# Three small clears behind each indirect transfer of a sparse MoE kernel

## The chip, the cores and the metric

The kernel runs on one core of a Trainium2 chip. The metric is the device time of one execution in microseconds (us). Where several runs are given, their median counts.

## What is computed

The input x has 2048 tokens of 256 numbers in float32. Two layers follow each other, and each has a feed-forward part before and after its middle part, added with half weight:

- Layer 0: a mixture of experts (8 experts with 176 hidden units, the best 2 for each token, and a shared expert), then a time mix and a channel mix, then the mixture again.
- Layer 1: a mixture of experts (32 experts with 96 hidden units, the best 6, and a shared expert), then attention with rotary angles over two sequences of 1024 tokens, then the mixture again.

One mixture, cut down from the reference:

```
scores = softmax(x @ gate_w);  topk_w, topk_idx = top_k(scores, K)
g = silu(x @ w_gate[e]) * (x @ w_up[e])            # for each expert e of a token
routed = sum over e of comb[t, e] * (g @ w_down[e])
shared = silu(x @ sw_gate) * (x @ sw_up) @ sw_down
out = routed + shared
```

In layer 1 the scores are sigmoids, and the K weights are scaled to a sum of one.

## The kernel before

The tokens lie in 16 tiles x0 to x15 of 128 rows, which stay in SBUF from start to end. The work is a sequence of mixtures with other parts between them. The two mixtures of layer 0, named L0_0 and L0_1, take all 16 tiles. Those of layer 1 are cut into halves A (tiles 0 to 7) and B (tiles 8 to 15): L1_0A, L1_0B, L1_1A, L1_1B. The profile shortens these names, to L, L_0A and so on.

A mixture computes only the chosen pairs of token and expert. Its steps, all functions inside `sparse_moe`:

1. `ready(g)`, for each of two groups of tiles: `prep` normalizes the tiles, transposes them, and picks experts; `plan` counts and gives every pair a slot (`idx`), so that slots of one expert lie together in blocks of 128; `scatter` writes each token's row to its slots in a DRAM tensor `xs`, with one indirect transfer of 128 rows (128 KB) for every tile and every k, issued by GpSimd (POOL).
2. `owners` and `weights` find which expert owns each block, and the weight of each pair.
3. `shared` computes the shared expert for a range of tiles.
4. `blocks` runs over the blocks (39 in layer 0, 79 in each half of layer 1). `fetch` loads a block of `xs` through SP's queue, and waits for all writes of step 1; `features` transposes it, `inner` and `outward` are the expert's matmuls (lines 600 and 617), and SP stores the result to a DRAM tensor `ys` (line 626).
5. `combine` reads the results back: `gather` issues, for each tile and k, one indirect transfer of 128 rows from `ys` into a tile `yk` (8 buffers) on POOL (line 636), and `add_back` adds it to x on DVE (line 647), four transfers later. A read for a tile of the first group needs the first 23 (layer 0) or 55 (layer 1) blocks to be stored, one for the second group needs all.

The parts overlap: the blocks of one half run while the other half's tokens are read back, attended and written. At the end nothing is left beside the reads of L1_1B but the last blocks.

There are 512 indirect transfers: 256 that write slots (32 + 32 + 4 x 48) and 256 that read (the same numbers). POOL does little else: constants and three zero tiles at line 282, and 32 additions to x in layer 0 (lines 829 and 851). An indirect transfer waits on POOL for its indices or for the blocks' stores; POOL takes its instructions in the order in which they stand in its queue.

The order of instructions on each engine is made by a scheduler, which simulates the program with costs of its own (`tc.block(schedule_with_timeline_sim=True)`), so a change can move instructions of other engines too. `tc.issue_after(x)` is a hint to it: what is issued inside stands behind x. It adds no wait on the chip.

Of the kernel before, what the change touches and what calls it, by code (L numbers as in the profile page):

```python
# [8 lines left out]
F32 = mybir.dt.float32  # L9
# [5 lines left out]
P = 128  # L15
# [24 lines left out]
def moe_blocks(m, tiles=NT):  # L40
    return (tiles * P * m["K"] + m["E"] * (P - 1)) // P
# [3 lines left out]
def macaron_kernel(ctx: ExitStack, tc: tile.TileContext, a: dict, out: bass.AP):  # L45
    nc = tc.nc
    ctx.enter_context(tc.block(schedule_with_timeline_sim=True))

    const = ctx.enter_context(tc.tile_pool(name="const", bufs=1))
# [220 lines left out]
    def load_down(w, layer, lo, n):  # L270
# [5 lines left out]
            ),  # L276
        )

    def fill_slots(xs, n, behind=None):

        zero = const.tile([P, D], F32, tag="zero", name=f"zero_{n}")
        nc.gpsimd.memset(zero, 0.0)
        d = nc.sync.dma_start(
            out=xs.rearrange("(n p) d -> p n d", p=P),
            in_=zero.unsqueeze(1).to_broadcast([P, n, D]),
        )
        if behind is not None:
            tc.add_manual_dep(d.ins, behind.name, SYNC, reason="not beside the blocks' loads")
# [6 lines left out]
    def sparse_moe(layer, w, name, first_tile, tiles, xs, ys, moe, last=False):  # L295
# [14 lines left out]
        idx = back.tile([P, tiles, K], I32, tag="idx", name=f"idx_{name}", bufs=2)  # L310
# [5 lines left out]
        def places(t):  # L316

            h, i = divmod(t, HT)
            if h not in xn:
                xn[h] = moe.tile([P, HT, D], F32, tag="xn", name=f"xn_{name}_{h}", bufs=2)  # L320
                xT[h] = moe.tile([P, DC, SEQ], F32, tag="xT", name=f"xTs_{name}_{h}", bufs=2)
            return xn[h], xT[h], i
# [109 lines left out]
        def scatter(g):  # L432

            for t in range(GT * g, GT * g + GT):
                xb, _, i = places(t)
                for k in range(K):
                    d = nc.gpsimd.indirect_dma_start(  # L437
                        out=xs,
                        out_offset=bass.IndirectOffsetOnAxis(ap=idx[:, t, k : k + 1], axis=0),
                        in_=xb[:, i, :],  # L440
                        in_offset=None,
                    )
                    tc.declare_no_dep(
                        d.ins, group=f"slots_{name}", reason="a slot is one pair's"
                    )
                    tc.add_to_no_dep_group(f"slots_{name}", d.ins)
                    scattered.append(d.ins)
# [183 lines left out]
        def gather(t, k):  # L631

            yk = back.tile([P, D], F32, tag="yk", name=f"yk_{name}_{t}_{k}", bufs=8)

            n = first if t < GT else NBLK
            d = nc.gpsimd.indirect_dma_start(  # L636
                out=yk,
                out_offset=None,
                in_=ys[0 : n * P, :],
                in_offset=bass.IndirectOffsetOnAxis(ap=idx[:, t, k : k + 1], axis=0),  # L640
            )
            for s in stored[0:n]:
                tc.add_manual_dep(d.ins, s.name, SYNC, reason="the blocks are done")
            gathered[t, k] = yk
# [10 lines left out]
        def combine(t0, t1, lag=4):  # L655

            pairs = [(t, k) for t in range(t0, t1) for k in range(K)]
            for n in range(len(pairs) + lag):
                if n < len(pairs):
                    gather(*pairs[n])  # L660
                if n >= lag:
                    add_back(*pairs[n - lag])
                yield
# [16 lines left out]
        def ready(g):  # L680

            for b in range(GT // BT * g, GT // BT * (g + 1)):
                prep(b)
            plan(g)
            scatter(g)
# [329 lines left out]
    xs, ys = {}, {}  # L1015
    for k, layer, tiles in (("L0", "L0", NT), ("A", "L1", HT), ("B", "L1", HT)):
        n = moe_blocks(MOE[layer], tiles)
# [8 lines left out]
    def rest_of_x():  # L1026
        for b in range(1, NB):
            load_x(b)
        fill_slots(xs["L0"], moe_blocks(MOE["L0"]))
# [8 lines left out]
    with tc.tile_pool(name="rwkvw", bufs=1) as weights:  # L1038
        with tc.tile_pool(name="moe_L0_0", bufs=1) as pool:
            m = sparse_moe("L0", w0, "L0_0", 0, NT, xs["L0"], ys["L0"], pool)  # L1040
            m["ready"](0)
            m["ready"](1)
            m["owners"]()
            load_rwkv(weights)
            m["weights"](0)
            m["weights"](1)
            m["shared"](0, HT)
            m["shared"](HT, NT)
            blocks = m["blocks"]()
            for n, _ in enumerate(blocks):  # L1050
                if n == m["first"] + 4:
                    break
            all_of(m["combine"](0, HT), blocks)
        all_of(m["combine"](HT, NT))
        for k in ("A", "B"):
            fill_slots(xs[k], moe_blocks(MOE["L1"], HT), behind=m["latest"]["add"])
        with tc.tile_pool(name="rwkv", bufs=1) as pool:
            rw["pool"] = pool
            run(rwkv)
# [121 lines left out]
```

## Time and profile before

| what | value |
|---|---|
| three runs | 1573.4, 1567.35 and 1575.41 us |
| median | 1573.4 us |
| profiled execution, own time | 1867.49 us |
| its span | 1865.7 us |
| granted clock of TensorE, mean | 0.814 |
| indirect transfer on POOL | 0.95 to 0.97 us, and 0.30 us until the next |
| POOL busy | 521.9 us (28%), 560 instructions |

The profiled execution is 294 us longer than the median of the timed runs. The profile names the engines PE (TensorE), PEld (its weight loads), DVE (VectorE), ACT (ScalarE), POOL (GpSimd) and SP. A row of a timeline has start and length in us, engine, line, operation, written and read tiles and shapes, and in brackets the idle time before it and what ended it. "remote", and "another core or an unknown queue" in the chain of waits, mean that the profile found nobody who ended the wait. The profile gives one execution, and the ends of matmuls in it are modelled.

### The profile page before, as it was taken

Reading aid. Unit: us, or ns where it says so; the run is one execution under the profiler, and the core shown is the slowest. Engines: PE = TensorE matmul, PEld = TensorE weight load, DVE = VectorE, ACT = ScalarE, POOL = GpSimd, SP = SyncE. Lnnn points to the kernel's source line nnn. Section 1 sums busy time; section 2 is a strip of 40 time slices with the busy share of each in tenths; the row PEclk is TensorE's granted clock in tenths of the full one; section 3 lists DMA queues with packets and bytes.
Section 4 is the critical chain, followed back from the end, with each engine's and each line's share of the span. In section 5 each row is a group of like instructions: output and inputs, shape, how many; then the busy total and the mean of one; then the engine's idle time right before and its main releaser. Section 6 shows DMA issues by size and latency. Waiting matters only on the chain.

```text
span 1865.7 us, 23891 instructions
## 1 busy us (share of the span) xinstructions
PE 1392.4 (75%) x6460; PEld 1080.6 (58%) x6460; DVE 763.6 (41%) x2586; ACT 660.8 (35%) x1796; POOL 521.9 (28%) x560
## 2 busy tenths in 40 slices
PE   6799767999879964634499758559778549788971
PEld 5577534566667743424398636449645439667960
DVE  5223368453322342233244554424446324344443
ACT  4133357775313330210154313126323216434520
POOL 1500331011060037236302340630540440342054
PEclk8699878999769975765699877679888559898985
DMA  9403339000720332172166420246631135555653
GB/s 280 162 27 107 105 124 371 18 1 0 155 85 29 105 93 101 68 200 79 62 187 184 135 60 23 96 137 187 172 96 31 65 107 179 175 158 165 186 173 102
DMA packets 204987, 223.54 MB, mean 120 GB/s; under 512 B 42268, under 2 KB 187836, under 8 KB 204860
## 3 DMA queue, kind: packets, MB, share of 16 engines
q1 hardware_dynamic: 180284, 154.87, 27.3%
q0 software_dynamic: 24576, 67.14, 11.5%
q8 instruction: 59, 0.97, 0.2%
q14 instruction: 68, 0.56, 0.1%
HBM read 108.81 MB, written 113.12 MB: 119 GB/s over the span
## 4 chain that ended last, share of the span: by engine, by line
PE 59%; another core or an unknown queue 13%; DVE 10%; issue 8%; ACT 5%; DMA 3%; POOL 1%; SPq 0%; POOLq 0%; DVEq 0%; ACTq 0%
PE pg_L_b L600 5%; PE pg_L L513 4%; PE py_L_b L617 3%; PE pkv_cm L761 3%; PE pg_L_1A_b L600 3%; PE pg_L_1B_b L600 3%; PE pg_L_0B_b L600 3%; PE pg_L_0A_b L600 3%; PE py_L L554 2%; PE pkk_cm L749 2%; PE py_L_1A_b L617 2%; PE py_L_1B_b L617 2%; PE py_L_0B_b L617 2%; PE py_L_0A_b L617 2%
## 5 line engine op out<-in xcount | busy, mean ns | idle before, releaser
L636 POOL DMA_INDIRECT yk_L<-ys_L,idx_L x64 | 62.2, 972 | 316.7 <-DMA ys_L<-yb_L 263.2
L600 PE MATMUL pg_L_b<-L0gu,xbT_L 128*128 x312 | 111.2, 481 | 0.0
L513 PE MATMUL pg_L<-L0sgu,xTs_L 128*128 128x352 f32 x256 | 99.1, 523 | 2.5 <-DVE h_L L504 2.5
L617 PE MATMUL py_L_b<-L0down,hT_L_b 88*128 x312 | 86.7, 403 | 10.6 <-ACT hT_L_b L536 6.2
L636 POOL DMA_INDIRECT yk_L_0A<-ys_A,idx_L_0A x48 | 46.1, 961 | 147.3 <-DMA ys_A<-yb_L_0A 103.2
L437 POOL DMA_INDIRECT xs_L<-xn_L,idx_L x64 | 61.7, 964 | 80.8 <-DVE wk_L L498 34.8
L617 PEld LDWEIGHTS py_L_b<-L0down,hT_L_b 88*128 88x128 f32 x312 | 62.2, 202 | 33.8 <-ACT hT_L_b L536 7.6
L636 POOL DMA_INDIRECT yk_L_1A<-ys_A,idx_L_1A x48 | 45.8, 954 | 124.4 <-DMA ys_A<-yb_L_1A 78.2
L636 POOL DMA_INDIRECT yk_L_0B<-ys_B,idx_L_0B x48 | 46.6, 970 | 121.0 <-DMA ys_B<-yb_L_0B 79.3
L504 DVE TENSOR_TENSOR h_L_b<-g_L_b,pg_L_b 128x176 f32<-128x176 f32 x78 | 26.2, 336 | 130.7 <-ACT g_L_b L503 104.9
L636 POOL DMA_INDIRECT yk_L_1B<-ys_B,idx_L_1B x48 | 46.0, 959 | 111.3 <-DMA ys_B<-yb_L_1B 89.4
L600 PE MATMUL pg_L_1A_b<-L1gu,xbT_L_1A 128*128 x316 | 69.9, 347 | 4.3 <-issue 3.9
L600 PE MATMUL pg_L_0B_b<-L1gu,xbT_L_0B 128*128 x316 | 70.5, 349 | 3.5 <-issue 3.1
L437 POOL DMA_INDIRECT xs_A<-xn_L_1A,idx_L_1A x48 | 46.7, 973 | 83.8 <-DVE same_L_1A L491 69.8
L437 POOL DMA_INDIRECT xs_B<-xn_L_1B,idx_L_1B x48 | 46.4, 967 | 81.9 <-DVE same_L_1B L491 67.8
L600 PE MATMUL pg_L_1B_b<-L1gu,xbT_L_1B 128*128 x316 | 68.8, 343 | 0.1
L600 PE MATMUL pg_L_0A_b<-L1gu,xbT_L_0A 128*128 x316 | 67.9, 339 | 0.2 <-PE ph_L_0A_b L529 0.2
L513 PEld LDWEIGHTS pg_L<-L0sgu,xTs_L 128*128 128x128 f32 x256 | 52.3, 219 | 26.1 <-issue 9.6
L600 PEld LDWEIGHTS pg_L_b<-L0gu,xbT_L 128*128 128x128 f32 x312 | 56.2, 199 | 18.4 <-issue 2.5
L536 ACT COPY hT_L_b<-ph_L_b 88x256 f32<-88x256 f32 x78 | 28.6, 369 | 103.7 <-PE ph_L_b L529 50.1
L617 PE MATMUL py_L_0B_b<-L1down,hT_L_0B_b 96*128 x158 | 51.5, 409 | 17.6 <-issue 11.9
L749 PE MATMUL pkk_cm<-mk_cm,w_WkeyT 128*128 128x512 f32 x128 | 60.8, 606 | 3.1 <-ACT sk_cm L841 3.1
(593 smaller groups left out, 3583.4 us busy)
## 6 DMA issues: line engine op xcount, KB each, us to landing
xs_A<-zero SPq DMA_DIRECT2D x1, 10112.0 KB
xs_B<-zero SPq DMA_DIRECT2D x1, 10112.0 KB
xb_L_0A<-xs_A SPq DMA_DIRECT2D x79, 128.0 KB
ys_A<-yb_L_0A SPq DMA_DIRECT2D x79, 128.0 KB
xb_L_0B<-xs_B SPq DMA_DIRECT2D x79, 128.0 KB
ys_B<-yb_L_0B SPq DMA_DIRECT2D x79, 128.0 KB
xb_L_1A<-xs_A SPq DMA_DIRECT2D x79, 128.0 KB
ys_A<-yb_L_1A SPq DMA_DIRECT2D x79, 128.0 KB
```

Source lines behind the costliest of these rows:

```text
L437: d = nc.gpsimd.indirect_dma_start(out=xs, out_offset=bass.IndirectOffsetOnAxis(ap=idx[:, t, k : k + 1], axis=0), in_=xb[:, i, :], in_offs ...
L504: nc.vector.tensor_tensor(dst, g, pg[:, width : 2 * width], ALU.mult)
L513: nc.tensor.matmul(pg, xbT[:, c, i * P : (i + 1) * P], w["sgu"][:, c, u, :, :].rearrange("p z w -> p (z w)"), start=(c == 0), stop=(c == D ...
L536: nc.scalar.copy(hT[0:m, lo:hi, :].rearrange("p k t -> p (k t)"), pt[0:m, lo * P : hi * P])
L554: nc.tensor.matmul(py, hT[0:m, k, :], w["sdown"][0:m, k, :], start=(k == 0), stop=(k == len(rows) - 1),)
L600: nc.tensor.matmul(pg, xbT[:, c, :], w["gu"][:, c, bass.ds(e, 1), :, :].rearrange("p e z h -> p (e z h)"), start=(c == 0), stop=(c == DC - 1),
L617: nc.tensor.matmul(py, hT[0:HP, k, :], w["down"][:, bass.ds(e, 1), k, :].rearrange("p e d -> p (e d)"), start=(k == 0), stop=(k == C - 1),)
L636: d = nc.gpsimd.indirect_dma_start(out=yk, out_offset=None, in_=ys[0 : n * P, :], in_offset=bass.IndirectOffsetOnAxis(ap=idx[:, t, k : k + ...
L749: nc.tensor.matmul(ps, w[:, c, oc * P : (oc + 1) * P], src[:, c, :], start=(c == 0), stop=(c == DC - 1),)
L761: nc.tensor.matmul(ps, src[:, c, i * P : (i + 1) * P], w[:, c, :], start=(c == 0), stop=(c == n - 1),)
```

## The change

A tile `pause` of 128 x 128 float32 is added. A helper `spaced` puts three clears of it on POOL behind each indirect transfer, and asks the scheduler to put the next transfer of the same kind (same mixture, and for writes the same group) behind the third. The writes of all mixtures go through it, and the reads of all but L1_1B.

```diff
+    pause = const.tile([P, P], F32, tag="pause", name="pause")
+
+    pauses = {}
+
+    def spaced(of, d):
+
+        if of in pauses:
+            with tc.issue_after(pauses[of]):
+                d = d()
+        else:
+            d = d()
+        with tc.issue_after(d.ins):
+            for _ in range(3):
+                pauses[of] = nc.gpsimd.memset(pause, 0.0).ins
+        return d
...
-                    d = nc.gpsimd.indirect_dma_start(
+                    d = spaced(("xs", name, g), lambda: nc.gpsimd.indirect_dma_start(
                         out=xs,
                         out_offset=bass.IndirectOffsetOnAxis(ap=idx[:, t, k : k + 1], axis=0),
                         in_=xb[:, i, :],
                         in_offset=None,
-                    )
+                    ))
...
-            d = nc.gpsimd.indirect_dma_start(
-                out=yk,
-                out_offset=None,
-                in_=ys[0 : n * P, :],
-                in_offset=bass.IndirectOffsetOnAxis(ap=idx[:, t, k : k + 1], axis=0),
-            )
+
+            def row():
+                return nc.gpsimd.indirect_dma_start(
+                    out=yk,
+                    out_offset=None,
+                    in_=ys[0 : n * P, :],
+                    in_offset=bass.IndirectOffsetOnAxis(ap=idx[:, t, k : k + 1], axis=0),
+                )
+
+            d = row() if name == "L1_1B" else spaced(("yk", name), row)
```

## The prediction

> **What bounds the kernel now.** I read the busy times and the chain of waits on the page first, then the stages by windows, then the timeline of one stage with many indirect transfers. In the page, PE carries the chain, and a line of the chain has no owner:
>
> ```profile
> span 1865.7 us, 23891 instructions
> PE 1392.4 (75%) x6460; PEld 1080.6 (58%) x6460; DVE 763.6 (41%) x2586; ACT 660.8 (35%) x1796; POOL 521.9 (28%) x560
> PE 59%; another core or an unknown queue 13%; DVE 10%; issue 8%; ACT 5%; DMA 3%; POOL 1%; SPq 0%; POOLq 0%; DVEq 0%; ACTq 0%
> ```
>
> There is one core, so 13% of 1865.7, 243 us, are waits that the profile cannot explain. The windows show where they lie (columns: PE, PEld, DVE, ACT, POOL busy, clock, DMA share, GB/s):
>
> ```profile
> 685.00:765.00 80.00, 33.19 (x130) 25.80 (x128) 22.90 (x120) 10.06 (x15) 48.46 (x51) 0.52 0.25 87
> 950.00:1000.00 50.00, 50.00 (x321) 46.40 (x320) 21.39 (x72) 27.36 (x107) 0.00 (x0) 1.00 0.62 190
> 1250.00:1300.00 50.00, 50.00 (x320) 45.19 (x319) 23.84 (x71) 31.33 (x107) 0.00 (x0) 1.00 0.61 186
> ```
>
> Where POOL issues nothing, PE is busy all of the time at full clock. Where POOL issues indirect transfers back to back, PE does 33 us of work in 80. The timeline of such a burst:
>
> ```profile
> 745.65 2.07 PE L617 MATMUL py_L_b<-L0down,hT_L_b 88*128 x4 [3.93 <-issue]
> ...
> 747.94 2.55 PE L600 MATMUL pg_L_b<-L0gu,xbT_L 128*128 x4
> ...
> 755.48 0.96 POOL L437 DMA_INDIRECT xs_A<-xn_L_0A,idx_L_0A  x1 [0.30 <-issue]
> 756.46 0.42 DVE L625 COPY yb_L<-py_L_b 128x256 f32<-128x256 f32 x1 [9.70 <-remote]
> 756.75 0.96 POOL L437 DMA_INDIRECT xs_A<-xn_L_0A,idx_L_0A  x1 [0.31 <-issue]
> ...
> 766.26 0.32 ACT L503 ACTIVATE g_L_b<-pg_L_b 128x176 f32<-128x176 f32 x1 [19.36 <-remote]
> ```
>
> DVE may copy py_L_b when its matmuls end at 747.7 and starts at 756.5; ACT may read pg_L_b at 750.5 and starts at 766.3. Counted over the timeline, a DVE or ACT instruction that needs a matmul's result starts more than 1 us late 63 times of 280 inside bursts and 5 times of 1317 outside; the late stretches together cover 284 us. Now the timed runs: the profiled execution took 1867.5 us, the median is 1573.4, 294 less. PE idles 1865.7 - 1392.4 = 473 us in the profile; a run of 1573 has room for 181 us of idling, and 473 - 284 is 189. I read this so: **the late starts belong to the profiled execution and are nearly all absent when the kernel is timed.** The trace's own records say the same: inside bursts it holds 429 semaphore events for 774 DVE instructions, outside 1530 for 1485. [...] So the sum below is made on the profile with the late starts taken out.
>
> [...] the row of 740.29 ends at 741.25, its semaphore rises at 742.52. [...]
>
> **The change part by part.** It adds 3 memsets behind 464 of the 512 indirect transfers: 256 writes to xs_* and 208 reads of ys_*; the 48 reads of sequence 1B stay. That is 1392 memsets. POOL's rows for the same shape:
>
> ```profile
> 1.39 0.20 POOL masks.py:65 MEMSET before<- 128x128 f32 x1
> 1.53 0.19 POOL L80 MEMSET every<- 128x128 f32 x1
> ```
>
> They start 0.14 us apart and take 0.20 each. In the program as built each memset also waits for the semaphore of the one before it. Three cost at least 3 x 0.14 = 0.42 us; at most 3 x (0.20 + 0.10) = 0.90 with a tenth for each wait. I take 0.14 + 2 x 0.20 = 0.54, about 0.55, since the first can start in the 0.30 us that POOL leaves idle behind each transfer. The interval of a burst is 0.96 + 0.30 = 1.27 us and becomes **1.82 us** (1.69 to 2.17). POOL gains 1392 x 0.2 = 278 us of work beside 522: it is never full over the span, so only ends of bursts count. Stage by stage:
>
> - First writes of L0_0 (32, from 40 us) end at 40 + 32 x 1.82 = 98 instead of 89.5. Shared-expert matmuls cover them to about 131 in the profile, 113 without 18 us of late starts: 0. L0_1 (32, from 513): 571 instead of 560.5; cover to 598 - 25 = 573, and data need 2 us to land: +0 (+11 at 2.17). In both, the built order puts the first write of group 1 ahead of the last four of group 0, so POOL waits there for group 1's indices; they are ready by then.
> - Reads of L0 before the time mix: the 16 late ones end 9 us later, at 277; POOL's first add behind them ran at 292. +2 for DVE's queue.
> - **From L0 to L1.** 16 reads from 667.6 end at 697 instead of 687.5; then 48 writes to xs_A, of which the built order puts 13 behind a read that needs the last L0 block. PE's blocks end at 800, of which 41 us are late starts between 685 and 765, so near 763. SP then loads L1down and attention weights for 23 us before the first xb_L_0A, so PE resumes at about 787. (In the built order SP's first nine loads of xb_L_0A move behind all eight turn tables, some 5 us, which the wait for the reads hides.) After: idx at 704, 35 writes to 768, one read, 13 writes to 793, then 15 reads to 821. Preparing half B needs 8 reads (808, against 790) and then all 16 (824, against 820 from its own pace): +18 and +4. **+22** (15 to 47).
> - Reads of 0A and 0B: 24 for group 0, then 24 for group 1, which attention's second half needs. For 0A, without late starts: group 0 from 1013.5 to 1057; group 1 may start at 1058 and ends at 1102 instead of 1088; with landing, adding and normalizing, 1108 against 1096, when PE is done with the first half. **+12 to 13 each, 26 together** (16 to 56).
> - Nothing for the writes of 0B, 1A and 1B and the reads of 1A: 112 us of block matmuls (79 x 1.42) stand between them and their use. If that cover went, each would cost 48 x 0.55 = 26 us.
>
> The sum is 0 + 2 + 22 + 26 = 50 us, 33 at the low price, about 119 at the high one. On the median: 1573.4 + 50 = **1623.4 us**.
>
> **Rivals.** *Faster, by fewer late starts.* If the timed run holds some of them, which needs PE's half-clock stretches to be faster there, the 189 us of other idling could shrink and leave up to 100 us of late starts. A first late start comes some 14 us into a burst (212 in the one from 197.6, 1028 in the one from 1013.5), as if something filled up; 0.55/1.82 = 30% fewer transfers per time could empty it. Then perhaps 60 of 100 us come back, and late starts being cover, only 30 of the 50 are paid: 1543 us. It decides once more than 50 us come back. For it: the burst is the only thing all late starts share. Against: the arithmetic of 294 and 284 us.
> *No change.* The scheduler sees the memsets and orders around them (PE has some 300 lines of difference in 5430 instructions), and the two exposed places shrink to a few us: 1578 us. Against: POOL's order of transfers is nearly the same, and PE's order at the two places too.
> *High price.* If each memset pays its semaphore in full, 2.17 us: 1692 us.
> *Not done as said.* The scheduler could have collected the memsets elsewhere; the built order has three between nearly all pairs, so this is left out. Less strain on the shared DMA engines brings nothing: PE is full at a DMA share of 0.62.
>
> **How the numbers follow.** Slower by the sum, 0.60; high price, 0.10; no change, 0.07; faster, 0.23. The likeliest's own range is 1600 to 1660. The range of 1540 to 1680 leaves out the best of the faster cases and the worst of the slow ones, about 2 in 10. 0.5% is 8 us, about what the three runs spread (8.06), and all that a measurement here can tell.
>
> **What would show it.** In the profile after, intervals in bursts of 1.8 us with three memset rows; xs_A's writes broken by a read and ending 30 us later against the gathers before; PE waiting for pt_L_0B and for the second pt_at group. The profiled execution itself may well get shorter[...], while the timed run gets longer. If the timed run gets shorter, the late starts were real, and the reading of 294 us is wrong; if nothing moves, the covers are longer than I put them.

## The result, and the profile after

| runs | before, median us | after, median us | ratio of after to before (95%) |
|---|---|---|---|
| the pair that gives the result (4 runs each) | 1571.81 | 1674.03 | 1.0654 [1.0622, 1.0686] |

On chips like the one that ran this pair, the change makes the kernel 102 us slower: the predicted direction, and a loss twice the forecast of 50 us. Its profiled execution took 1673.05 us, as much as its timed runs; that of the kernel before had taken 1867.49 against a median of 1573.4.

The head of the page after, its chain by engine, and the row of the clears (busy us, mean ns | idle before):

```profile
span 1671.3 us, 25279 instructions
...
PE 1336.4 (80%) x6460; PEld 1045.6 (63%) x6460; DVE 767.9 (46%) x2586; ACT 665.4 (40%) x1796; POOL 818.9 (49%) x1952
...
PE 54%; DMA 15%; DVE 10%; POOL 9%; issue 6%; ACT 4%; SPq 2%; POOLq 0%; DVEq 0%; ACTq 0%
...
L292 POOL MEMSET pause<- 128x128 f32 x1392 | 292.7, 210 | 54.0
```

"Another core or an unknown queue" has gone from the chain; DMA and POOL have taken 12 and 8 points more. Not all of this is the change: the experiments show that the two profiles are of chips of different kinds. The windows of two bursts of 48 writes (columns as before), xs_A of L1_0A and xs_B of L1_1B:

```profile
669.00:764.00 95.00, 50.05 (x222) 38.24 (x222) 29.86 (x123) 17.03 (x44) 78.15 (x193) 0.70 0.49 148
1334.00:1424.00 90.00, 83.22 (x499) 74.48 (x498) 48.84 (x183) 46.63 (x151) 75.58 (x189) 0.90 0.63 200
```

In the second, PE works through the burst (83 of 90 us busy). In the first it still has a hole (50 of 95), and the waits say why (us in total, times, longest):

```profile
PE pt_at L148 <- DVE axl_at L139: 51.3, 2, 26.3
PE px_L_0A L594 <- DMA xb_L_0A<-xs_A: 43.4, 2, 42.7
PE pt_L_0A L148 <- DVE xn_L_0A L139: 19.8, 2, 16.2
PE pt_L_0B L148 <- DVE xn_L_0B L139: 15.7, 2, 12.7
```

These are not late starts but waits for the end of a burst: the first block of L1_0A for the last write to xs_A, and the second half of attention, twice, for the reads of 0A and of 0B. Counted as in the prediction, a start over 1 us late comes 2 times in 903 inside bursts, where it was 63 in 280; here too the chips differ. The price of three clears, in POOL's timeline: a burst of writes, then one of reads:

```profile
699.21 0.97 POOL L453 DMA_INDIRECT xs_A<-xn_L_0A,idx_L_0A  x1 [0.16 <-issue]
700.18 0.74 POOL L292 MEMSET pause<- 128x128 f32 x3
701.09 0.97 POOL L453 DMA_INDIRECT xs_A<-xn_L_0A,idx_L_0A  x1 [0.16 <-issue]
...
940.88 0.95 POOL L654 DMA_INDIRECT yk_L_0A<-ys_A,idx_L_0A  x1 [0.50 <-issue]
941.83 0.74 POOL L292 MEMSET pause<- 128x128 f32 x3
943.07 0.95 POOL L654 DMA_INDIRECT yk_L_0A<-ys_A,idx_L_0A  x1 [0.50 <-DVE h_L_0A_b L520]
```

A write now starts 1.88 us after the one ahead, a read 2.19; the prediction took 1.82 for both. In place of 0.30 us of idling stand 0.74 + 0.16 = 0.90 behind a write and 0.74 + 0.50 = 1.24 behind a read, so three clears cost 0.60 and 0.94 us.

### The profile page after: what moved, and what is told of

It reads as the page before. It is cut to its first block, busy times and chain, and to the rows that moved or that the text cites. A ratio compares the mean times of both kernels' runs of the same rounds, so it can differ in the third digit from the quotient of the medians.

```text
span 1671.3 us, 25279 instructions
## 1 busy us (share of the span) xinstructions
PE 1336.4 (80%) x6460; PEld 1045.6 (63%) x6460; DVE 767.9 (46%) x2586; ACT 665.4 (40%) x1796; POOL 818.9 (49%) x1952
## 4 chain that ended last, share of the span: by engine, by line
PE 54%; DMA 15%; DVE 10%; POOL 9%; issue 6%; ACT 4%; SPq 2%; POOLq 0%; DVEq 0%; ACTq 0%
PE pg_L_b L616 5%; PE pg_L L529 4%; POOL pause L292 4%; PE py_L_b L633 4%; PE pkv_cm L781 3%; DMA yk_L<-ys_L,idx_L 3%; PE py_L L570 3%; PE pg_L_1A_b L616 3%; DMA yk_L_1A<-ys_A,idx_L_1A 2%; PE pg_L_0B_b L616 2%; DMA yk_L_0B<-ys_B,idx_L_0B 2%; PE pkk_cm L769 2%; PE pg_L_0A_b L616 2%; DMA yk_L_0A<-ys_A,idx_L_0A 2%; PE pg_L_1B_b L616 2%
## 5 line engine op out<-in xcount | busy, mean ns | idle before, releaser
L292 POOL MEMSET pause<- 128x128 f32 x1392 | 292.7, 210 | 54.0
L529 PE MATMUL pg_L<-L0sgu,xTs_L 128*128 128x352 f32 x256 | 92.9, 499 | 3.8 <-DVE h_L L520 3.8
L633 PE MATMUL py_L_b<-L0down,hT_L_b 88*128 x312 | 81.8, 385 | 0.0
L520 DVE TENSOR_TENSOR h_L_b<-g_L_b,pg_L_b 128x176 f32<-128x176 f32 x78 | 26.2, 336 | 95.4 <-ACT g_L_b L519 95.1
L616 PE MATMUL pg_L_0B_b<-L1gu,xbT_L_0B 128*128 x316 | 66.3, 333 | 0.5 <-issue 0.2
L616 PE MATMUL pg_L_1A_b<-L1gu,xbT_L_1A 128*128 x316 | 65.6, 331 | 0.8 <-PE ph_L_1A_b L545 0.7
L594 PE MATMUL px_L_0A<-ident,xb_L_0A 128*128 128x128 f32 x158 | 30.9, 280 | 43.4 <-DMA xb_L_0A<-xs_A 43.4
L654 POOL DMA_INDIRECT yk_L_1A<-ys_A,idx_L_1A x48 | 46.7, 973 | 36.6 <-DMA xb_L_1A<-xs_A 12.4
L667 DVE SCALAR_TENSOR_TENSOR x<-yk_L,wk_L,x 128x256 f32<-128x256 f32 x64 | 30.8, 481 | 70.6 <-DMA yk_L<-ys_L,idx_L 70.2
```

The costliest lines, as they stand in the source:

```text
L292: pauses[of] = nc.gpsimd.memset(pause, 0.0).ins
L520: nc.vector.tensor_tensor(dst, g, pg[:, width : 2 * width], ALU.mult)
L529: nc.tensor.matmul(pg, xbT[:, c, i * P : (i + 1) * P], w["sgu"][:, c, u, :, :].rearrange("p z w -> p (z w)"), start=(c == 0), stop=(c == D ...
L594: nc.tensor.transpose(px[:, c * P : (c + 1) * P], xb[:, c * P : (c + 1) * P], ident)
L616: nc.tensor.matmul(pg, xbT[:, c, :], w["gu"][:, c, bass.ds(e, 1), :, :].rearrange("p e z h -> p (e z h)"), start=(c == 0), stop=(c == DC - 1),
L633: nc.tensor.matmul(py, hT[0:HP, k, :], w["down"][:, bass.ds(e, 1), k, :].rearrange("p e d -> p (e d)"), start=(k == 0), stop=(k == C - 1),)
```

## The experiments

All variants edit the helper `spaced`; most leave some transfers without clears:

```diff
     def spaced(of, d):
 
+        if not (<the transfers that keep their clears>):
+            return d()
         if of in pauses:
```

In these runs the kernel before turned out to have two times, by the chip that ran it, and the ratio always compares runs of one chip:

| set, chip | kernel | before us | this us | ratio (95%) |
|---|---|---|---|---|
| 1, chip 12 | e1_covered: writes 0B, 1A, 1B, reads 1A | 1855.98 | 1724.17 | 0.9272 [0.9246, 0.9298] |
| 1, chip 12 | e2_turn: reads L0_1, writes L1_0A | 1855.98 | 1836.33 | 0.9901 [0.9867, 0.9936] |
| 1, chip 12 | e3_attend: reads L1_0A, L1_0B | 1855.98 | 1868.96 | 1.0065 [1.0041, 1.0088] |
| 1, chip 12 | e4_layer0: writes and reads L0_0, writes L0_1 | 1855.98 | 1823.80 | 0.9829 [0.9805, 0.9853] |
| 2, chip 13 | e5_after: the whole change | 1572.35 | 1674.69 | 1.0661 [1.0595, 1.0726] |
| 2, chip 13 | e6_one: one clear, not three | 1572.35 | 1566.64 | 0.9970 [0.9951, 0.9989] |
| 2, chip 13 | e8_before: the kernel before, profiled | 1572.35 | 1568.43 | one run |
| 3, chip 9 | e9_spared: all but those of e2 and e3 | 1574.11 | 1590.20 | 1.0098 [1.0059, 1.0136] |
| 3, chip 9 | e10_one: one clear | 1574.11 | 1567.33 | 0.9949 [0.9930, 0.9967] |
| 3, chip 9 | e11_attend: as e3 | 1574.11 | 1625.34 | 1.0301 [1.0248, 1.0355] |
| 3, chip 9 | e12_after: the whole change | 1574.11 | 1675.88 | 1.0635 [1.0593, 1.0677] |
| 4, chip 2 | e13_turn: as e2 | 1867.96 | 1850.28 | 0.9914 [0.9885, 0.9943] |

### The change cut into four places

```diff
# e1_covered
+        if not (of[:2] in (("xs", "L1_0B"), ("xs", "L1_1A"), ("xs", "L1_1B"), ("yk", "L1_1A"))):
# e2_turn
+        if not (of[:2] in (("yk", "L0_1"), ("xs", "L1_0A"))):
# e3_attend
+        if not (of[:2] in (("yk", "L1_0A"), ("yk", "L1_0B"))):
# e4_layer0
+        if not (of[:2] in (("xs", "L0_0"), ("yk", "L0_0"), ("xs", "L0_1"))):
```

> Clears only behind the 192 transfers that I held to be covered by block matmuls: the writes of L1_0B, L1_1A, L1_1B and the reads of L1_1A. Place theory (a longer burst is paid only where something waits for its end): 0 to +8 us against the kernel before. Rival, price per transfer wherever it lies [...]: 102 us x 192/464 = +42. In the profile, late starts vanish from these four bursts and stay in the others, so the profiled execution should come out roughly midway between 1867 and 1673 us while the timed runs stay near 1572.

> Clears only behind the 80 transfers of the passage from layer 0 to layer 1: the reads of L0_1 and the writes of L1_0A. Place theory with the waits of the profile after (PE stands 16, 5, 43, 13 and 5 us there, part of which the kernel before has too): +35 to +50 us; the prediction's own term was +22. Rival, price per transfer: 102 x 80/464 = +18.

> Clears only behind the 96 reads of L1_0A and L1_0B, ahead of attention. Place theory with the two waits for pt_at of 25 and 26 us in the profile after: +35 to +52 us; the prediction's own term was +26. Rival, price per transfer: 102 x 96/464 = +21.

> Clears only behind the 96 transfers of L0_0 (writes and reads) and the writes of L0_1. Place theory: +2 by the prediction, up to +20 by the four waits of PE of 25 us in all around the time mix in the profile after. Rival, price per transfer: 102 x 96/464 = +21. If places add up without touching each other, the four kernels of this set sum to the +102 us of the whole change.

All four expectations fell, and with them a premise of mine. The 13 runs of the kernel before took 1851 to 1865 us here: what I had thought a property of one profiled execution is the usual time here. There the clears behind the covered bursts gained 132 us, those of the turn 20 and of layer 0 32, and only attention's reads lost 13. Here is the profile of e1_covered, head and chain, and the windows of three bursts of 48 writes, of which the first (to xs_A of L1_0A) has no clears and the others (xs_B of L1_1B and of L1_0B) have them:

```profile
span 1730.1 us, 24471 instructions
...
PE 60%; DVE 9%; issue 8%; DMA 8%; another core or an unknown queue 6%; ACT 5%; POOL 2%; SPq 2%; DVEq 0%; POOLq 0%; ACTq 0%
```

```profile
704.00:766.00 62.00, 23.96 (x85) 17.50 (x85) 15.35 (x82) 3.09 (x5) 46.57 (x48) 0.53 0.29 104
1378.00:1469.00 91.00, 83.95 (x483) 74.99 (x482) 48.40 (x182) 45.16 (x145) 76.24 (x189) 0.86 0.60 193
854.00:947.00 93.00, 89.74 (x521) 79.93 (x522) 45.28 (x178) 40.80 (x150) 76.61 (x190) 0.90 0.58 186
```

The last of these bursts, on the same chip without clears, in e3_attend:

```profile
849.00:910.00 61.00, 21.35 (x80) 15.91 (x79) 14.81 (x78) 1.01 (x3) 46.11 (x48) 0.56 0.28 101
```

So the same 48 writes leave PE busy for 21 of 61 us without clears and for 90 of 93 with them. The gain is where the clears are: in the four bursts of e1_covered that have them, no start is over 1 us late. The late starts themselves are in the timeline of the burst without clears (the bracket is the idle time and what ended it):

```profile
756.05 0.96 POOL L455 DMA_INDIRECT xs_A<-xn_L_0A,idx_L_0A  x1 [0.30 <-issue]
...
758.42 0.42 DVE L643 COPY yb_L<-py_L_b 128x256 f32<-128x256 f32 x1 [9.65 <-issue]
...
769.62 0.32 ACT L521 ACTIVATE g_L_b<-pg_L_b 128x176 f32<-128x176 f32 x1 [20.73 <-remote]
```

The ACT instruction at this place had waited 19.36 us in the profile that the prediction used.

### The whole change, one clear, and the kernel before on another chip

```diff
# e6_one
-            for _ in range(3):
+            for _ in range(1):
```

> The whole change once more, on the chip of this set. The comparison of the first four variants had the kernel before at 1856 us, against 1572 in the pair of runs that gave the result. Theory D (the late starts belong to a condition of the chip or session, and where it holds they are in every execution): where the kernel before takes about 1856, this one takes 1670 to 1690 (ratio 0.90 to 0.91: the four parts sum to -132 -20 +13 -32 = -171), with no late starts left; where it takes about 1572, this one takes about 1674 (ratio 1.065). Rival (spacing costs the same 102 us everywhere, and the first four gains have another source): 1.055 where before takes 1856.

> The whole change with one clear in place of three. Interval of a burst 1.45 us by my estimate (0.97 for the transfer, 0.16 to the clear, 0.21 for it, some 0.1 to the next transfer), against 1.27 and 1.92. If late starts need a transfer rate above some limit and 1.45 us is already below it: 1600 to 1630 us on any chip, the best of the three. If 1.45 is not enough, late starts stay where the chip has them (1750 or more, when before takes 1856). Where before takes 1572: 1572 + 102 x 0.18/0.65 = 1600.

> The kernel before, profiled on the chip of this set. Theory D: where its timed runs take 1856, the profile holds some 63 late starts inside bursts; where they take 1572, it holds next to none, and PE's waits at the places of the change can be read from it directly.

On chip 13 the kernel before takes 1572 us, and here it is profiled at that speed: page, windows of the bursts of writes to xs_A and xs_B, and waits.

```profile
span 1566.6 us, 23891 instructions
...
PE 1330.9 (85%) x6460; PEld 1041.7 (66%) x6460; DVE 760.7 (49%) x2586; ACT 664.6 (42%) x1796; POOL 526.6 (34%) x560
...
PE 52%; DMA 12%; DVE 10%; ACT 5%; issue 4%; POOL 1%; SPq 0%; POOLq 0%; DVEq 0%; ACTq 0%
```

```profile
662.00:724.00 62.00, 50.10 (x213) 38.11 (x213) 26.11 (x113) 14.04 (x39) 46.59 (x48) 0.78 0.49 160
764.00:825.00 61.00, 57.70 (x320) 50.18 (x321) 32.48 (x135) 23.30 (x82) 46.33 (x48) 0.87 0.55 184
```

```profile
PE px_L_0A L578 <- DMA xb_L_0A<-xs_A: 24.7, 1, 24.7
PE pt_L_0A L148 <- DVE xn_L_0A L139: 12.5, 1, 12.5
...
PE pt_L_0B L148 <- DVE xn_L_0B L139: 7.7, 1, 7.7
PE pt_at L148 <- DVE axl_at L139: 5.9, 2, 2.9
```

The same program, with the same 48 writes at 1.27 us, has PE busy for 50 of 62 us and no unknown waits: 2 of 656 instructions in bursts start over 1 us late. So late starts belong neither to the program alone nor to the act of profiling alone: chip 12 has them (the rows of e1_covered above), chip 13 next to none, and by the time of the kernel before chip 2 goes with the first (1868 us) and chip 9 with the second (1574 us). Each chip was used in one session only, so a condition of the session is not told apart from the chip. The profile that the prediction was made on was, by its late starts, of the first kind, and the three timed runs beside it, by their time, of the second; on which chips they ran is not on record.

This makes a clean pair with e5_after on the same chip. Where PE stands at the same point of the work, in us from the start:

| PE reaches | before | after | behind |
|---|---|---|---|
| first transposes of L1_0A | 646.7 | 652.0 | 5.3 |
| first block of L1_0A | 739.3 | 765.0 | 25.7 |
| first transposes of L1_0B | 749.3 | 780.4 | 31.1 |
| attention over 0A, second half | 960.1 | 1022.6 | 62.5 |
| attention over 0B, second half | 1192.5 | 1281.9 | 89.4 |
| end of the last matmul | 1525.4 | 1627.0 | 101.6 |

The turn costs 26 us, attention 31 and 27, the start and the end 5 and 12. PE idles 90.1 us longer up to its last matmul (284.6 against 194.5) and is busy 11.5 us longer with the same 6460 matmuls, the mean granted clock being 0.860 against 0.884.

One clear costs nothing (1566.64 us against 1572.35). Its timeline shows why:

```profile
894.07 0.95 POOL L654 DMA_INDIRECT yk_L_0A<-ys_A,idx_L_0A  x1 [0.17 <-DVE yb_L_0A L641]
895.01 0.23 POOL L292 MEMSET pause<- 128x128 f32 x1
895.40 0.95 POOL L654 DMA_INDIRECT yk_L_0A<-ys_A,idx_L_0A  x1 [0.16 <-issue]
```

0.23 + 0.16 us replace the 0.30 us of idling, so a read comes every 1.33 us in place of 1.25, and the 48 reads of 0A, with the wait for the last block among them, take 75.3 us; in the kernel before they take 77.2. The expected +28 us, one clear as its share of the three, did not come. Why it is even slightly faster was not traced; PE is already 8 us ahead at the first transposes of L1_0A (638.3 against 646.7).

### The remaining places on an undisturbed chip

```diff
# e9_spared
+        if not (of[:2] not in (("yk", "L0_1"), ("xs", "L1_0A"), ("yk", "L1_0A"), ("yk", "L1_0B"))):
```

e10_one, e11_attend and e12_after repeat e6_one, e3_attend and e5_after.

> Clears behind all transfers of the change except the four bursts that PE waits for: no clears behind the reads of L0_1, the writes of L1_0A and the reads of L1_0A and L1_0B, so 288 of 464 keep them. From PE's idle stretches in the profiles of the same chip (kernel before and whole change): the spared places hold 16 + 5 + 4 us of the passage from layer 0 to layer 1 and 22 + 23 us of attention, 70 in all. Where the kernel before takes about 1572 us: place theory +5 to +25; rival, price per transfer, 102 x 288/464 = +63. Where it takes about 1856: the two variants with the same places gave -132 and -32, so 1680 to 1710.

> One clear in place of three, as in the set before (1.33 to 1.38 us between transfers, 0.997 of the kernel before where that takes 1572). Where the kernel before takes about 1856: if late starts need a rate above some limit between 1/1.27 and 1/1.92 and 1.35 us is already below it, about 1570 to 1600; if it is not, 1750 to 1850. Where it takes 1572: 0.997 again, 1560 to 1575.

> Clears only behind the 96 reads of L1_0A and L1_0B, as before. Where the kernel before takes about 1572: place theory +40 to +50, since a burst of 48 reads takes 103 us in place of 77 (25.5 longer, twice), and the two waits for pt_at are 24.9 and 26.2 us against 2.9 each; rival, price per transfer, +21. Where it takes 1856: 1.0065 again.

> The whole change. Where the kernel before takes about 1856: 1670 to 1690, faster by a tenth, since with 1.9 us between transfers no late starts are left and the time is that of the other chip. Where it takes 1572: 1.066 again.

The chip of this set, too, shows no late starts: the kernel before takes 1574 us, and none of the longest waits in the profiles of e9_spared and e11_attend ends on "remote". Clears on attention's reads alone cost 3.0%, 47 us (39 to 56): 46% of the loss from 21% of the transfers. (The medians are 51 apart, since one of the four runs took 3410.84 us; it counts in the median and is left out of the ratio.) Clears on the other 288 transfers cost 16 us (9 to 21), where a price per transfer asks for 63. So the loss is a matter of place. The two waits for attention stand at 25 and 26 us in the profile of e11_attend, and those of the turn as in the kernel before:

```profile
PE pt_at L148 <- DVE axl_at L139: 51.5, 2, 26.2
PE px_L_0A L596 <- DMA xb_L_0A<-xs_A: 25.8, 1, 25.8
```

In e9_spared both are as before (px_L_0A 25.3, pt_at 2.9 twice), and no single wait shows its 16 us: against e8_before PE is 6 us behind at the first transposes of L1_0A, 8 at the second half of attention over 0B, and 17 at the end, with 6 us more of busy PE.

> Clears only behind the reads of L0_1 and the writes of L1_0A, as in the first set. Where the kernel before takes about 1572 us: place theory by subtraction, 102 for the whole less 47 (attention's reads alone) less 16 (all but these places): +39; by PE's idle stretches alone (16 + 5 + 4 us more than before): +25; the prediction's own term: +22; rival, price per transfer: +18. Where the kernel before takes about 1856: 0.990 again, the gain on late starts in the two bursts against the same cost.

This run came to a chip with the long time (before: 1867.96 us) and gave 0.991, where e2_turn gave 0.990 on chip 12. In these two ratios a second chip behaves like the first. What the clears of the turn alone cost on an undisturbed chip was thus not measured; it is 26 us by PE's positions above and 39 by subtraction (102 - 47 - 16), whose terms are uncertain by 6 to 9 us each.

## Why the prediction was right, and where it was not

- **Direction and places: right.** The loss comes from longer bursts where something waits for their end, at the places named: the turn from layer 0 to layer 1 and attention's second half, twice. PE waits for pt_L_0B and pt_at as forecast, and xs_A's writes are broken by a read. That break cost little: in e5_after the 35th write starts at 734.6 and the 36th, behind the read, at 737.7, which is 1.2 us more than an interval. The size was too small: 1674 us is above the 1600 to 1660 that I held likeliest and 6 us inside the wide range: the sum of 50 us was half of the 102.
- **"The late starts belong to the profiled execution": wrong.** On two chips every execution of the kernel before takes the long time (24 runs of 1851 to 1874 us), on two others none of 38 does. The forecast held because the arithmetic needed only that the *timed* runs be free of them: 1867 less 294 us, which e8_before confirms with 1568 us and next to no late starts. That the pair was timed under that condition was luck. The match of 284 us of late starts with the missing 294 was luck as well: of the 299 us between the spans of the two profiles, PE's idling makes 238 (473 less 236), and 61 are a PE that is busy for less time (1392.4 against 1330.9), at a mean clock of 0.884 against 0.814. The rival "faster, by fewer late starts" had it right for the other chips: late starts went where the bursts were slower (none over 1 us is left in the four bursts of e1_covered that have clears), though nothing shows that something fills up, and the parts gained 132, 20 and 32 us and lost 13. They sum to -171, which would give some 1685 us for the whole change if they add up; the whole change was not run on such a chip.
- **The interval of 1.82 us: the mis-sized term.** I let the first clear hide in the 0.30 us of POOL's idling. It does start at once, but another 0.16 us follows the last clear behind a write and 0.50 behind most reads. For a write this comes to 0.60 us where I took 0.55; the miss is the read, at 0.94. The rival "high price" of 2.17 us is right for the reads (2.16 to 2.23 over a burst) and too high for the writes; its 1692 us is nearer than my 1623. Its tenth of a microsecond for the wait of each memset was my estimate: in the profile after, the second and the third clear start 0.06 us after the end of the one before.
- **Attention, +26 predicted:** 58 us by PE's positions, 47 (39 to 56) by e11_attend. The sum's own rule gives the size once the interval is right: at 1.82 us the first 24 reads end before the last block is stored, and only the second 24 count; at 2.19 the first 24 take 52 us, longer than the 45 that the blocks need (in e8_before the 25th read starts 44.5 us after the first), and all 48 run on end: 102.5 us against 77.2 for 0A and 104.3 against 75.3 for 0B. PE's two waits for pt_at so grow from 2.9 us each to 24.9 and 26.2, 45 us in all. Of the rest of the 58, 8 us come before attention over 0A begins: from the first transposes of L1_0B to there PE takes 193.5 us against 185.3. Why was not traced.
- **The turn, +22 predicted:** 26 us by PE's positions. It was sized about right, but not by the wait that the sum had. I put 18 of the 22 us on the preparation of half B; the traces put most on the first block of L1_0A, which needs the last write to xs_A: the 48 writes run from 668.1 to 761.5 us, PE gets the block at 765.0, and its wait there grows from 24.7 to 41.2 us, while the one for pt_L_0B grows only from 7.7 to 12.4.
- **Layer 0, +2, and "nothing" for the covered bursts:** 16 us by e9_spared. Most of the cover held: the four bursts are 125 us longer in all in e5_after than in e8_before. But the few us at the start and the end, and a PE that is busy longer at a lower mean clock (6 us more in e9_spared, at 0.878 against 0.884), were in no term of the sum. How much of the 16 comes from the longer bursts and how much from the changed order of other engines' instructions was not separated.
- **The profiled execution would shrink while the timed runs grow:** so it came out, 1867 to 1673 and 1572 to 1674, but this is no support for the reading that the late starts belong to the profiled execution: the two profiles were of chips of different kinds.
- **The no-change rival** fell: no place shrank to a few us. In the built programs, asking for the order alone, without any clears, gives the same order of instructions as the kernel before on every engine; so the clears themselves moved the other instructions. No such kernel was timed.

## What to carry to other kernels

When a profiled execution's own time is far from the timed median, first ask whether both were taken under the same conditions; profile the kernel again beside timed runs before a gain or a loss is built on the difference. A delay put into a long burst is worth computing in two steps: the new interval, from the idle time that the delay replaces and that which reappears behind it, and then, for each burst, who waits for its last element and whether its parts still wait for something else or now run on end. Where such a change gains on some chips and costs on others, its place and its size decide: left out of the four bursts that PE waits for, it cost 16 us in place of 102 on an undisturbed chip, and behind the covered bursts alone it gained 132 on a disturbed one. One clear in place of three made the kernel 0.3% to 0.5% faster ([0.9951, 0.9989] and [0.9930, 0.9967]), the best version of the study on undisturbed chips; it wasn't run on a chip with late starts.

## What the runs showed of the hardware that was not expected

- **One program, two times, by chip or session.** The kernel before takes 1856 and 1868 us on chips 12 and 2, and 1572 and 1574 on chips 13 and 9. The late starts that I could place are nearly all in bursts of indirect transfers at 1.25 to 1.27 us each (63 of 68 in the profile that the prediction used); in the burst of e1_covered shown above the DVE row starts 8.7 us, and the ACT row 17 us, after the matmuls that write its tile have ended (at 749.7 and 752.5). The DMA engines are not fuller there: a share of 0.29 in the burst without clears of e1_covered, 0.49 in the same burst of the kernel before on chip 13. With three clears, at 1.9 us for a write and 2.2 for a read, none over 1 us is left in the four bursts of e1_covered that have them.
- **The trace loses records on those chips.** On chip 13 the trace of the kernel before holds 8162 events of the eight semaphores on which the 512 transfers land, close to 16 for each; the profile that the prediction used holds 2013 of the same, and those of chips 12 and 2 hold 2604 to 2790. The profile after, without late starts but for 2 in 903, holds 8174. What the loss has to do with the late starts, no run here shows. The timed runs have a granted clock on record too, so none is known to have gone unrecorded: whether these chips would be slow without recording, and why only they are, stays open.
- **A second wait behind three clears goes with a third of a microsecond.** Behind most reads the idle time after three clears is 0.50 us, behind most writes 0.16; with one clear both have 0.16 or 0.17. The difference is not one of reads and writes. Where POOL's sequencer has one more wait for a semaphore between two transfers, as it has for most reads in the built program, the trace of e5_after shows about 0.50 us for 151 of 156 reads and 31 of 40 writes (that of the profile after for 153 of 156 and 30 of 39); where it has none, 41 of 42 reads and 209 of 212 writes start within 0.2 us. With one clear (e6_one) the same extra wait goes with no such delay: 156 of 158 reads start within 0.2 us. Why it takes three clears was not tested.
